# Row maxima in one, two, one chunk from the second batch on, turned in blocks, and an opening loaded through two queues

## The chip, the cores and the metric

The kernel runs on one core of a Trainium2 chip. The metric is the device time of one execution in microseconds (us), as the median of several runs. TensorE is called PE, VectorE DVE, ScalarE ACT, GpSimd POOL; SP is the engine whose queue issues most of the transfers.

## The reference

One transformer layer with normalisation after each half, on `x` of 4 batches x 512 rows x 512 features, in float32. All 16 heads (32 wide) share one key and one value head.

```python
q = rotary((x @ Wq + bq).reshape(B, T, H, HD).transpose(0, 2, 1, 3))
k, v = rotary((x @ Wk + bk)[:, None]), (x @ Wv + bv)[:, None]
attn = softmax(einsum("bhqd,bhkd->bhqk", q, k) / sqrt(HD))
x = layernorm(x + merge(attn @ v) @ Wo + bo)
hidden = sigmoid(x @ quant(w1).T) * (x @ quant(w2).T)      # 1408 wide
out = layernorm(x + hidden @ quant(w3).T)
# quant(w) = clip(round(w / (mean(abs(w)) + 1e-8)), -1, 1)
```

## The kernel before

The work is a list of 64 attention steps `(b, c, t)`: batch b, group c of four heads (NG = 4), key tile t of 128 keys. They are counted from 0 here, so batch b has steps 16b to 16b+15. A step computes the transposed scores of four heads against 128 keys in two PSUM tiles `ps` (tag `sc`, two buffers of two banks), subtracts each row's maximum with a second small matmul (`negm` against ones, adding into `ps`), takes the exponential on ACT (`es`), and one step later weighs the values (`weigh`, into `acc`). In batch 0 the denominators are also summed on PE (`count`, into the bank `den`); in later batches POOL adds them up (`total`), and DVE folds them (`part`).

The maxima must be known before the scores. So `find_maxima` computes, seven steps ahead (LEAD), the scores the other way round (`pmax`), and DVE reduces them to `mx`. In batch 0 this is `row_maxima`, two heads at a time; from batch 1 on it is `maximum`, for one head and some of its four chunks of 128 queries: a pair of chunks takes a `sc` buffer, a single chunk takes the one bank `den`. When a group's maxima are complete, `spread` turns them: PE transposes `mx` (128 x 16) into `pm`, a tile of `ps_mm` (tag `mm`, two banks), ACT and DVE split the negated maxima into two parts `m`, SP writes them to DRAM (`rows`) and reads them back as rows (`negm`).

Between the maxima, a step draws other work from a list, `fill`: in halves, the projections of later batches (`project_in`: `pk`, then `pq` for each of the four groups; after each, DVE rotates the result in four or five instructions, `turn`), the output projection (`po`) with its statistics, and the feed-forward part (`gu`, `po`, one batch behind the attention). `pace` says how much a step draws. `late` holds small jobs (`spread`, `normalize`, layer norms, stores) that `due` advances twice a step. All engines but SP's waits run their instructions in the order in which this program writes them: `InOrder` and `pin` keep it.

`quantized` goes through 66 weight tiles (33 twice): the first pass sums absolute values, the second takes a sign on ACT (`sgn`) and forms -1, 0 or 1 on DVE (into `raw`), and POOL stores them. `quantize(n)` advances it by n tiles. In steps after the 16th, the sign goes to the PSUM bank `den`.

Which form a step has is decided in the main loop: as long as the last batch isn't projected (`batches[-1].done < NC`, which holds up to step 25), it takes chunks (0, 1) and (2, 3) with all of the drawn work behind them; afterwards it takes 0, then 1 and 2, then 3, with work drawn between.

The opening issues every load on SP, in this order: two small biases, `wkv`, the four chunks of `xT` of batch 0, a part of `wq`, `cos`, `sin`, and the rest. Meanwhile PE runs WARM = 24 matmuls on ones. Line 75 is the helper that records ACT, DVE and POOL instructions, line 80 that of matmuls, line 83 that of SP's transfers, line 86 that of transposes.

Of the kernel before, what the change touches and what calls it, by code (L numbers as in the profile page):

```python
# [10 lines left out]
F32 = mybir.dt.float32  # L11
F32R = mybir.dt.float32r
BF16 = mybir.dt.bfloat16
I32 = mybir.dt.int32
AF = mybir.ActivationFunctionType
ALU = mybir.AluOpType
# [4 lines left out]
P = 128  # L21
HD = 32
# [6 lines left out]
def postln_block(  # L29
# [15 lines left out]
    nc = tc.nc  # L45
    B, T, D = x.shape
    NC = D // P
    NT = T // P
    NF = wf.shape[1]
    NG = P // HD  # L50
    SCALE = 1.0 / float(HD) ** 0.5
    W = 512
    WARM = 24

    const = ctx.enter_context(tc.tile_pool(name="const", bufs=1))
    small = ctx.enter_context(tc.tile_pool(name="small", bufs=2))
    work = ctx.enter_context(tc.tile_pool(name="work", bufs=2))
# [4 lines left out]
    dram = ctx.enter_context(tc.tile_pool(name="dram", bufs=1, space=DRAM))  # L62
    ps_sc = ctx.enter_context(tc.tile_pool(name="ps_sc", bufs=2, space=PSUM))
    ps_acc = ctx.enter_context(tc.tile_pool(name="ps_acc", bufs=1, space=PSUM))
    ps_mm = ctx.enter_context(tc.tile_pool(name="ps_mm", bufs=2, space=PSUM))

    pin = tc.keep_in_program_order
# [9 lines left out]
    act, dve, pool = InOrder(nc.scalar), InOrder(nc.vector), InOrder(nc.gpsimd)  # L77
# [4 lines left out]
    def move(out, in_):  # L82
        pin(nc.sync.dma_start(out=out, in_=in_))  # L83

    def transpose(out, in_, identity):
        pin(nc.tensor.transpose(out, in_, identity))

    ident = const.tile([P, P], F32, name="ident")
# [16 lines left out]
    bq_sb = const.tile([P, 2 * NC], F32, name="bq_sb")  # L105
    bkv_sb = const.tile([P, 2], F32, name="bkv_sb")
# [11 lines left out]

    chunks = iter([(b, c) for b in range(B) for c in range(NC)])

    def load_xT(n):

        for _ in range(n):
            b, c = next(chunks, (None, None))
            if b is not None:
                batches[b].xT.append(work.tile([P, T], F32, tag="xT", name="xT", bufs=6))
                move(batches[b].xT[c], xT[b, :, c, :])

    move(bkv_sb, bkv)
    move(bq_sb, bq)  # L130
    move(wkv_sb, wkv)
    load_xT(NC)
    move(wq_sb[0], wq[:, 0])
    move(cos_sb, cos)
    move(sin_sb, sin)
# [22 lines left out]
    def quantized():  # L158

        order = ((0, False), (1, False), (0, True), (2, False), (1, True), (2, True))
        jobs = [(m, last, f) for m, last in order for f in range(NF)]

        means = {}
        for n, (m, last) in enumerate(order):
            if not last:
                for k, step in ((2, 0), (6, 1), (10, 2)):
                    means[(n + 1) * NF + k] = (m, step)
        raws, part, row, pg, hi, waiting = {}, {}, {}, {}, {}, []  # L170

        def load(k):
            if k < len(jobs):
                m, _, f = jobs[k]

                tag, bufs = ("wd", 5) if k % 2 else ("wg", 4)
                raws[k] = wp.tile([P, W], F32, tag=tag, name="raw", bufs=bufs)
                pool.dma_start(out=raws[k], in_=wf[m, f])

        def mean(m, step):  # L180
            if step == 0:
                row[m] = small.tile([P, 1], F32, tag="row", name="row")
                dve.tensor_reduce(row[m], part[m], AX.X, ALU.add)
            elif step == 1:
                pg[m] = ps_mm.tile([P, 1], F32, tag="mm", name="pg")
                mm(pg[m], ones, row[m], True, True)
                gamma = small.tile([P, 1], F32, tag="gamma", name="gamma")
                act.activation(gamma, pg[m], AF.Identity, scale=1.0 / (NF * W * P), bias=eps_q)
                row[m] = gamma
            else:  # L190
                hi[m] = small.tile([P, 1], F32, tag="hi", name="hi")
                act.mul(hi[m], row[m], 0.5)

        AHEAD = 4
        for k in range(AHEAD):
            load(k)
        for k, (m, last, f) in enumerate(jobs):
            load(k + AHEAD)
            if k in means:
                mean(*means[k])  # L200
            raw = raws.pop(k)
            if not last:
                if f == 0:
                    part[m] = small.tile([P, NF], F32, tag="part", name="part", bufs=3)
                junk = work.tile([P, W], BF16, tag="th", name="junk")
                act.activation(junk, raw, AF.Abs, accum_out=part[m][:, f : f + 1])
            else:
                if now > PER:

                    sgn = ps_acc.tile([P, W], F32, tag="den", name="sgn")  # L210
                else:
                    sgn = work.tile([P, W], BF16, tag="th", name="sgn")
                act.activation(sgn, raw, AF.Sign, bias=hi[m])
                dve.scalar_tensor_tensor(raw, raw, hi[m], sgn, ALU.is_gt, ALU.min)
                waiting.append((kept[m][f], raw))
            if len(waiting) > 2 or k + 1 == len(jobs):
                for w, q in waiting[: 1 if k + 1 < len(jobs) else 3]:
                    pool.dma_start(out=w.bitcast(F32), in_=q)
                del waiting[:1]
            yield  # L220
# [164 lines left out]
    def spread(b, c):  # L385


        s = batches[b]
        pm = ps_mm.tile([NG * NT, P], F32, tag="mm", name="pm")
        transpose(pm, s.mx[c].rearrange("p i t -> p (i t)"), ident)  # L390
        m = small.tile([NG * NT, 2, P], F32R, tag="m", name="m")
        mH, mL = m[:, 0, :], m[:, 1, :]
        act.mul(mH, pm, -1.0)
        dve.scalar_tensor_tensor(mL, pm, -1.0, mH.bitcast(F32), ALU.mult, ALU.subtract)
        s.negm[c] = work.tile([P, T], F32R, tag="negm", name="negm", bufs=3)
        yield
        rows = dram.tile([2, NG, T], F32, tag="rows", name="rows", bufs=3)
        move(rows.rearrange("n i (t k) -> (i t) n k", k=P), m.bitcast(F32))
        yield
        for n in range(2):  # L400
            move(s.negm[c].bitcast(F32).rearrange("(i r) k -> i r k", r=HD)[:, n], rows[n])
        yield

    def scores(b, c, t):
# [372 lines left out]
    def quantize(n):  # L777
        for _ in range(n):
            next(weights, None)
# [12 lines left out]
    def due():  # L792

        nonlocal slot
        slot += 1
        for entry in list(late):
            if slot >= entry[0] and next(entry[1], "end") == "end":
                late.remove(entry)
# [13 lines left out]
    def find_maxima(k, *chunks):  # L812

        if k >= len(steps):
            return
        b, c, i = steps[k]
        if chunks[0] == 0:
            ask(k + HEADS)
            while batches[b].done <= c or (b and k not in heads):
                if batches[b].done <= c:  # L820
                    fill.one()
                else:
                    begin_middle()
                    due()
                    ask(k)
        if b == 0:
            row_maxima(b, c, i, chunks[0] // 2)
        else:
            maximum(b, c, i, chunks, heads[k])
        if i == NG - 1 and chunks[-1] == NT - 1:  # L830

            late.insert(0, (slot + (1 if now < 0 else 2), spread(b, c)))
# [22 lines left out]
    for n, (b, c, t) in enumerate(steps):  # L855
        now = n
        pace = (1.8, 3.8, 4.8, 4.6)[b]
        if t == 1 and PER <= n + NT - 1 < len(steps):
            load_q(*steps[n + NT - 1][:2])
        es = scores(b, c, t)  # L860
        if last is not None:
            weigh(*last)
        if last is not None and last[0] == 0:
            count(*last)
        last = (b, c, t, es)
        if n == NC * NT // 2:

            late.append((slot, load_x(0)))
        if t == NT - 1:
            begin = slot + 3  # L870
            late.append((begin, normalize(b, c)))
            if c == NC - 1:
                late.append((begin + 7, feed(b)))
                if b > 0:
                    late.append((slot + 6, load_x(b)))
        if batches[-1].done < NC:

            find_maxima(n + LEAD, 0, 1)
            begin_middle()
            due()  # L880
            find_maxima(n + LEAD, 2, 3)
            quantize(1)
            fill.draw(pace)
            quantize(1 if b == 0 or n % 3 == 0 else 0)
        else:
            find_maxima(n + LEAD, 0)
            fill.draw(0.4 * pace)
            find_maxima(n + LEAD, 1, 2)
            begin_middle()
            due()  # L890
            fill.draw(0.3 * pace, True)
            find_maxima(n + LEAD, 3)
            fill.draw(0.3 * pace)
        due()
# [70 lines left out]
```

## Time and profile before

| | |
|---|---|
| median of 3 runs | 672.12 us (670.8 to 674.28) |
| the profiled execution | 672.56 us, its span 670.8 us |
| mean granted TensorE clock | 0.997 |
| instructions | 9406 |
| PE, DVE, ACT, POOL busy | 644.7, 430.0, 282.8, 324.4 us |
| HBM read, written | 84.06 MB, 23.10 MB |

The span runs from the first to the last instruction. Busy times are unions; a matmul's row shows the time until its result is written, and matmuls overlap, so the distance between starts says more of PE's pace than the durations do. In a row of groups come line, engine, operation, output<-input, shapes, count, then busy us and mean ns of one, then the idle time of the engine just before and what ended it. In a row of the timeline come start, length, engine, line, operation, names, shapes, count, and in brackets the idle time before. In a row of the windows come the stretch, its length, the busy time of each engine, the granted clock, the mean share of the DMA engines, and GB/s.

### The profile page before, as it was taken

Reading aid. Unit: us, or ns where it says so; the run is one execution under the profiler, and the core shown is the slowest. Engines: PE = TensorE matmul, PEld = TensorE weight load, DVE = VectorE, ACT = ScalarE, POOL = GpSimd, SP = SyncE. Lnnn points to the kernel's source line nnn. Section 1 sums busy time; section 2 is a strip of 40 time slices with the busy share of each in tenths; the row PEclk is TensorE's granted clock in tenths of the full one; section 3 lists DMA queues with packets and bytes.
Section 4 is the critical chain, followed back from the end, with each engine's and each line's share of the span. In section 5 each row is a group of like instructions: output and inputs, shape, how many; then the busy total and the mean of one; then the engine's idle time right before and its main releaser. Section 6 shows DMA issues by size and latency. Waiting matters only on the chain.

```text
span 670.8 us, 9406 instructions
## 1 busy us (share of the span) xinstructions
PE 644.7 (96%) x3222; PEld 358.5 (53%) x3222; DVE 430.0 (64%) x619; ACT 282.8 (42%) x441; POOL 324.4 (48%) x414
## 2 busy tenths in 40 slices
PE   9989999999999989999999899999999999999995
PEld 6333333443333355665456466654555685778884
DVE  1896766587787867766666966676635553464335
ACT  1466555655443644333334445233435421234213
POOL 0615334535987776376666375576574802202000
PEclk9999999999999999999999999999999999999998
DMA  8755668688575286355132456351232364236531
GB/s 283 248 192 175 205 199 261 186 286 276 162 245 172 92 259 202 116 169 162 54 84 82 125 164 215 124 172 29 73 100 67 126 217 148 79 109 213 183 107 63
DMA packets 60671, 107.78 MB, mean 161 GB/s; under 512 B 14592, under 2 KB 15360, under 8 KB 60624
## 3 DMA queue, kind: packets, MB, share of 16 engines
q1 hardware_dynamic: 52560, 81.10, 38.5%
q0 software_dynamic: 7920, 25.96, 11.8%
q8 instruction: 25, 0.41, 0.3%
q14 instruction: 22, 0.18, 0.1%
q10 hardware_dynamic: 144, 0.13, 0.1%
HBM read 84.06 MB, written 23.10 MB: 160 GB/s over the span
## 4 chain that ended last, share of the span: by engine, by line
PE 81%; DVE 9%; DMA 4%; ACT 3%; issue 2%; SPq 1%; POOL 0%; DVEq 0%; ACTq 0%; POOLq 0%
PE gu L80 23%; PE po L80 19%; PE ps L80 11%; PE pmax L80 8%; PE acc L80 7%; PE pq L80 7%; DVE mx L75 3%; PE den L80 2%; DMA wg<-w 2%; ACT es L75 2%; PE pk L80 1%; DVE xt L75 1%; PE warm L80 1%; SPq L83 1%; DMA xT<-in_xT 1%
## 5 line engine op out<-in xcount | busy, mean ns | idle before, releaser
L75 DVE TENSOR_REDUCE mx<-pmax 128x1 f32<-128x512 f32 (+1 forms) x159 | 158.1, 1007 | 81.3 <-PE pmax L80 81.1
L75 ACT ACTIVATE es<-ps 128x1024 f32<-128x1024 f32 x128 | 124.2, 1022 | 141.9 <-PE ps L80 133.9
L80 PE MATMUL gu<-y,wg 128*128 128x512 f32 x704 | 172.9, 395 | 2.0 <-DMA wg<-w 1.1
L80 PEld LDWEIGHTS gu<-y,wg 128*128 128x128 f32 x704 | 131.1, 188 | 38.4 <-issue 4.7
L75 POOL TENSOR_TENSOR total<-total,es 128x512 f32<-128x512 f32 x96 | 123.8, 1319 | 45.2 <-ACT es L75 45.1
L80 PE MATMUL po<-wd,h 128*128 128x512 f32 x352 | 87.0, 395 | 4.2 <-DVE y L75 2.9
L75 POOL TENSOR_TENSOR total<-es 128x512 f32<-128x512 f32 x48 | 60.5, 1290 | 55.8 <-ACT es L75 55.8
L80 PE MATMUL pmax<-kr,qr 128*128 128x512 f32 x192 | 75.2, 455 | 3.7 <-ACT es L75 2.2
L80 PEld LDWEIGHTS po<-wd,h 128*128 128x128 f32 x352 | 64.9, 188 | 22.5 <-DVE y L75 4.6
L75 ACT CAST h<-hw 128x512 fp32r<-128x512 f32 x44 | 27.3, 620 | 100.7 <-DVE hw L75 100.7
L80 PE MATMUL acc<-es,v 128*32 128x512 f32 x512 | 68.2, 605 | 0.0
L80 PEld LDWEIGHTS pmax<-kr,qr 128*128 128x128 f32 x192 | 33.6, 188 | 57.0 <-ACT es L75 20.9
L75 DVE SCALAR_TENSOR_TENSOR hw<-th,gu 128x512 f32<-128x512 f32 x44 | 30.2, 687 | 46.9 <-PE gu L80 46.8
L80 PE MATMUL po<-wo_sb,ctxT 128*128 128x512 f32 x128 | 58.9, 593 | 0.3 <-DVE hw L75 0.3
L80 PE MATMUL ps<-negm,ones_r 2*128 2x512 f32 x256 | 58.2, 788 | 0.0
L75 DVE SCALAR_TENSOR_TENSOR xt<-po,xt 128x512 f32<-128x512 f32 x48 | 32.8, 684 | 38.1 <-PE po L80 38.1
L75 DVE TENSOR_TENSOR h<-hw,h 128x512 fp32r<-128x512 f32 x44 | 42.1, 957 | 21.7 <-ACT h L75 21.4
L80 PE MATMUL ps<-qT,kT 32*128 32x512 f32 x384 | 55.6, 640 | 0.0
L75 POOL DMA_DIRECT2D raw<-in_wf x66 | 36.1, 549 | 37.4 <-DMA w<-raw 26.7
L80 PE MATMUL pq<-xT,wq_sb 128*128 128x512 f32 x112 | 53.0, 601 | 1.0 <-ACT v L75 1.0
L75 ACT ACTIVATE th<-gu 128x512 f32<-128x512 f32 x44 | 26.3, 598 | 49.1 <-PE gu L80 49.0
L80 PEld LDWEIGHTS po<-wo_sb,ctxT 128*128 128x128 f32 x128 | 24.1, 189 | 22.0 <-issue 19.2
(98 smaller groups left out, 639.2 us busy)
## 6 DMA issues: line engine op xcount, KB each, us to landing
wg<-w SPq DMA_DIRECT2D x88, 256.0 KB
raw<-in_wf POOLq DMA_DIRECT2D x66, 256.0 KB, 4.6
qr<-qp SPq DMA_DIRECT2D x96, 128.0 KB
wd<-w SPq DMA_DIRECT2D x44, 256.0 KB
w<-raw POOLq DMA_DIRECT2D x33, 256.0 KB, 4.9
qp<-q SPq DMA_DIRECT2D x48, 128.0 KB
rden<-flat SPq DMA_DIRECT2D x64, 64.0 KB
xt<-in_x SPq DMA_DIRECT2D x16, 256.0 KB
```

Source lines behind the costliest of these rows:

```text
L75: return lambda *args, **kw: pin(getattr(self.engine, name)(*args, **kw))
L80: pin(nc.tensor.matmul(out, lhsT=lhsT, rhs=rhs, start=start, stop=stop))
L83: pin(nc.sync.dma_start(out=out, in_=in_))
```

## The change

Five things change.

- WARM goes from 24 to 10.
- The four opening chunks of `xT` are issued alternately by ACT's queue and SP's; the two bias loads follow on ACT's queue.
- `spread` no longer uses PE and ACT: DVE negates the 128 x 16 maxima, takes the rest, and turns both in blocks of 32 x 32 (`turned`). The rows go to DRAM as 128 pieces of 128 bytes, and `negm` is put together from pieces of 128 bytes.
- The steps' form: all steps from batch 1 on take chunk 0, then 1 and 2, then 3, with work drawn between. By the built order this affects steps 16 to 25; before and after them the steps hold the same work in the same order, but for `spread`.
- From step 17 on the sign of the quantizing goes to an SBUF buffer (`rot_a`, bfloat16) in place of the bank `den`, which the single chunks now use.

```diff
-    WARM = 24
+    WARM = 10
...
-    def load_xT(n):
+    def load_xT(n, engines=(nc.sync,)):
...
-        for _ in range(n):
+        for k in range(n):
...
-                move(batches[b].xT[c], xT[b, :, c, :])
-
-    move(bkv_sb, bkv)
-    move(bq_sb, bq)
+                pin(engines[k % len(engines)].dma_start(out=batches[b].xT[c], in_=xT[b, :, c, :]))
+
     move(wkv_sb, wkv)
-    load_xT(NC)
+    load_xT(NC, (nc.scalar, nc.sync))
+    pin(nc.scalar.dma_start(out=bkv_sb, in_=bkv))
+    pin(nc.scalar.dma_start(out=bq_sb, in_=bq))
...
-                    sgn = ps_acc.tile([P, W], F32, tag="den", name="sgn")
+                    sgn = work.tile([P, W], BF16, tag="rot_a", name="sgn", bufs=1)
...
-        pm = ps_mm.tile([NG * NT, P], F32, tag="mm", name="pm")
-        transpose(pm, s.mx[c].rearrange("p i t -> p (i t)"), ident)
-        m = small.tile([NG * NT, 2, P], F32R, tag="m", name="m")
-        mH, mL = m[:, 0, :], m[:, 1, :]
-        act.mul(mH, pm, -1.0)
-        dve.scalar_tensor_tensor(mL, pm, -1.0, mH.bitcast(F32), ALU.mult, ALU.subtract)
+        mx = s.mx[c].rearrange("p i t -> p (i t)")
+        m = small.tile([P, 2, NG * NT], F32R, tag="m", name="m")
+        turned = small.tile([P, HD], F32, tag="turned", name="turned")
+        dve.tensor_scalar(m[:, 0, :], mx, -1.0, None, ALU.mult)
+        dve.scalar_tensor_tensor(m[:, 1, :], mx, -1.0, m[:, 0, :].bitcast(F32), ALU.mult, ALU.subtract)
+        dve.transpose(turned, m.rearrange("p n k -> p (n k)").bitcast(F32))
         s.negm[c] = work.tile([P, T], F32R, tag="negm", name="negm", bufs=3)
         yield
-        rows = dram.tile([2, NG, T], F32, tag="rows", name="rows", bufs=3)
-        move(rows.rearrange("n i (t k) -> (i t) n k", k=P), m.bitcast(F32))
-        yield
+        rows = dram.tile([P // HD, 2, NG, NT, HD], F32, tag="rows", name="rows", bufs=3)
+        move(rows.rearrange("o n i t k -> (o n i t) k"), turned)
+        yield
+        to = s.negm[c].bitcast(F32).rearrange("(i r) (t o k) -> i r t o k", r=HD, t=NT, o=P // HD)
         for n in range(2):
-            move(s.negm[c].bitcast(F32).rearrange("(i r) k -> i r k", r=HD)[:, n], rows[n])
+            move(to[:, n], rows[:, n].rearrange("o i t k -> i t o k"))
...
-        if batches[-1].done < NC:
+        if b == 0:
 
             find_maxima(n + LEAD, 0, 1)
             begin_middle()
...
             find_maxima(n + LEAD, 0)
+            quantize(1)
             fill.draw(0.4 * pace)
             find_maxima(n + LEAD, 1, 2)
             begin_middle()
             due()
+            quantize(1 if n % 3 == 0 else 0)
             fill.draw(0.3 * pace, True)
```

## The prediction

> **What bounds the kernel now.** I read the page's busy shares first, then the chain that ended last, then the groups kept apart by shape, the timeline of single steps, and the windows of the opening.
>
> ```profile
> PE 644.7 (96%) x3222; PEld 358.5 (53%) x3222; DVE 430.0 (64%) x619; ACT 282.8 (42%) x441; POOL 324.4 (48%) x414
> ...
> PE 81%; DVE 9%; DMA 4%; ACT 3%; issue 2%; SPq 1%; POOL 0%; DVEq 0%; ACTq 0%; POOLq 0%
> ```
>
> TensorE (PE) is busy for 96% of the span and carries 81% of the chain: what leaves its queue, or makes it wait, moves the end; other engines matter only where they hold it up.
>
> ```profile
> L80 PE MATMUL pmax<-kr,qr 128*128 128x512 f32 x192 | 75.2, 455 | 3.7 <-ACT es L75 2.2 <-DVE mx L75 1.0
> L86 PE MATMUL pm<-ident,mx 128*16 128x128 f32 x16 | 4.4, 273 | 1.3 <-DVE mx L75 1.3
> L75 DVE SCALAR_TENSOR_TENSOR m<-pm,m 16x128 fp32r<-16x128 f32 x16 | 4.3, 270 | 0.0
> ```
>
> These groups are touched. Waits are small throughout; the 16 `pm` transposes cost PE 273 ns each before what follows them is counted.
>
> **Part 1, the opening: -3.4 us.** In the windows (PE first, then the loads; last the granted clock, DMA share, GB/s):
>
> ```profile
> 1.50:7.30 5.80, 5.80 (x27) 5.80 (x28) 0.00 (x0) 0.71 (x2) 0.16 (x3) 1.00 0.74 177
> 7.30:9.80 2.50, 2.50 (x24) 2.50 (x24) 0.00 (x0) 0.00 (x0) 0.00 (x0) 1.00 1.03 354
> 9.80:13.30 3.50, 3.50 (x11) 1.59 (x10) 0.00 (x0) 0.00 (x0) 0.00 (x0) 1.00 1.05 406
> ```
>
> The 24 warming matmuls are 48 passes, and the first real one, `pk`, starts at 9.77 with no wait shown: it stands behind the warming. Passes come every 0.215 us up to 7.3 (5.80/27) and every 0.104 us after it (2.50/24), although the granted clock reads 1.00: PE runs at half pace first. Ten warming matmuls are 20 passes and end near 5.9. The data: by the windows of one microsecond some 0.9 MB had landed by 7.0 and 1.6 MB by 9.0. `wkv` and the first `xT` chunk are 0.52 MB, so about 5.1, all four chunks 1.3 MB, about 8.2. The two small bias loads go off SP's front, so everything is issued 0.9 us earlier (`wkv` from 1.64 to 0.73): 4.2 and 7.3. The last chunk is needed 2.6 us after `pk` starts, so data aren't late. ScalarE's four issues, at about 0.45 us each by SP's rows, are hidden: its first real work starts at 13.40 now. `pk` thus moves from 9.77 to 5.9, 3.8 us. Until about 7.3 it runs at half pace, which loses 0.7 us; if the pace doubles earlier, nothing. I take -3.4. Bounds: -3.8, and -0.4 if all of `pk` (3.44 us now) runs at half pace.
>
> [...]
>
> **Part 2, the first turned maxima: -0.3.** At 37 us VectorE (DVE) sets the pace: PE's `pm` waits 1.26 us for `mx`, the next maxima come late, and DVE idles 0.49 us before 38.39. That gap goes; two more small DVE instructions come. Nearest rows: 160 ns (128x1 product), 246 (reciprocal 128x16), 233 (block transpose 32x64). Three for one of 270 ns is +0.2 to +0.5. Net -0.3 (0 to -0.4).
>
> **Part 3, the other transposes: -5.6.** After batch 0's opening, four lie in batch 0, three in steps 16 to 25 (part 4), eight later. Step 28, without, takes 244.52 to 251.61, 7.09 us; step 29, with the same matmuls and `pm`, 251.61 to 259.41, 7.80: 0.71 more, for `pm` also takes one of two PSUM banks and the next `gu` waits (0.28). The last is followed by a wait of 0.68. At 0.6 each: 4.8. In batch 0 the next matmul starts 0.03 to 0.21 after `pm`: 0.2 each, 0.8. DVE's extra 0.2 to 0.5 is hidden in the late steps, where it idles 1.2 to 4 us (6.58 busy of 7.80 in step 29), and mostly in batch 0 (0.1 to 1.1 idle); without that cover it costs up to 0.6 there. Bounds: 12 x 0.27 less 0.6 = 2.6, and 6.5; a loss is excluded, since PE's own time goes in any case. The longer DMA route (128 pieces of 128 bytes) is hidden: the maxima leave at 258.42, are fetched at 262.72 and needed at 273.6; three times that latency fits.
>
> [...]
>
> **Part 4, steps 16 to 25: +5.1, a loss.** Only these ten change their chunks; later steps had one, two, one already. A step now, then one of the later kind:
>
> ```profile
> 171.89 0.81 PE L80 MATMUL ps<-negm,ones_r 2*128 2x512 f32 x4
> 172.63 1.07 PE L80 MATMUL acc<-es,v 128*32 128x512 f32 x8
> 173.80 0.73 PE L80 MATMUL pmax<-kr,qr 128*128 128x512 f32 x2
> 174.72 0.73 PE L80 MATMUL pmax<-kr,qr 128*128 128x512 f32 x2 [0.18 <-ACT es L75]
> 175.29 1.88 PE L80 MATMUL pq<-xT,wq_sb 128*128 128x512 f32 x4
> ...
> 245.82 1.07 PE L80 MATMUL acc<-es,v 128*32 128x512 f32 x8
> 246.81 0.50 PE L80 MATMUL pmax<-kr,qr 128*128 128x512 f32 x1
> 247.16 2.02 PE L80 MATMUL gu<-y,wg 128*128 128x512 f32 x8
> 249.02 0.63 PE L80 MATMUL pmax<-kr,qr 128*128 128x512 f32 x2
> 249.48 1.98 PE L80 MATMUL gu<-y,wg 128*128 128x512 f32 x8
> 251.30 0.39 PE L80 MATMUL pmax<-kr,qr 128*128 128x512 f32 x1
> ```
>
> Gains: `acc` and maxima take 2.66 us (172.63 to 175.29) against 0.99+0.35+0.46+0.31 = 2.11, less seams 0.5 a step; nine steps 4.5. Three `pm` at 0.35: 1.0. Two waits (0.38 on `xT`, 0.35 on `v`) vanish under new ones: 0.7. Together 6.2.
>
> Losses: DVE's queue. Now the maxima are reduced before the rotation of the projection:
>
> ```profile
> 174.57 2.36 DVE L75 TENSOR_REDUCE mx<-pmax 128x2 f32<-128x1024 f32 x2 [0.29 <-PE pmax L80]
> 176.85 0.74 DVE L75 SCALAR_TENSOR_TENSOR raw<-raw,hi,sgn 128x512 f32<-128x512 f32 x1
> 177.50 0.74 DVE L75 SCALAR_TENSOR_TENSOR a<-pq,bq_sb,cos_sb 128x512 f32<-128x512 f32 x1
> ```
>
> Afterwards, by the built order, the fill between chunk 0 and the pair puts the rotation ahead of the pair's reduce in steps 16 to 19. The pair's bank of `sc` is also the one that the next step's second `ps` needs, and behind that `ps` stands all of PE. If the fill ends at F, the rotation runs from F+0.2 for 2.9 us (177.50 to 180.44) and the reduce 1.2: free at F+4.3. PE reaches the second `ps` at F+2.9 (pair 0.46, another fill half 1.8, chunk 3 0.32, first `ps` 0.28), or F+1.1 without that half. Step 16: 1.4. Step 17 rotates `pk`, after `kv` (0.68) and for 3.6 us: free at F+5.7, 2.8. Step 18, with `pv`: 1.0. Step 19, no second half: 3.2. Also, in step 16 chunk 0 takes the `den` bank, which ScalarE's `sums` copy frees: 159.36 now, behind a sign of 0.75 then, so 160.1; PE is there at 158.4: 1.7. In steps 20, 21 and 24 chunk 3's reduce stands behind statistics and `part` or `m`: 0.4 each, 1.2. Together 11.3. Net +5.1. Bounds: -0.5 if half of the waits come, +10 below. The signs' move to SBUF costs ScalarE 0.03 us each (693 ns into PSUM, 720 into SBUF) on an engine busy 42%; one buffer as before.
>
> **Sum.** -3.4 -0.3 -5.6 +5.1 = -4.2 on the profiled execution's 672.56 (span 670.8 and 1.76 around it): 668.4. That execution is 0.44 over the median 672.12, so **667.9**. Half a per cent, 3.4 us, is about what a measurement can tell from no change.
>
> **Rivals.**
> - *The rotation waits half vanish* (part 4 at -0.5): 662.3. For it: PE had only 0.2 to 0.65 us of idle in each of these steps. Against: both queues are strictly in order. 0.17.
> - *The opening brings little* (-0.4), PE staying at half pace because it stops after the warming, that is, the shorter warming doesn't do what it says: 670.9. Against: the data are there. 0.13.
> - *Slower: the one shared bank.* Chunk 0 of the next step waits for chunk 3's reduce too. If that also slips behind a rotation in 16 to 19, 4 x 2.9 = 11.6 more: 679.5. It decides from 7.6 us more. For it: DVE is busy 7.96 of 8.50 us in step 18 now. Against: the built order has that reduce directly after the pair's, or after one sign product. 0.15.
>
> **Numbers.** The forecast has 0.55, its own range 665.5 to 670.5; three quarters of it lie below 668.7, so 0.41 faster and 0.14 same. Faster 0.41+0.17 = 0.58; same 0.14+0.13 = 0.27; slower 0.15. Reaching from the first rival to half way to the third, with 2 in 10 outside: 663.0 to 674.5.
>
> **What would show it.** `pk` starting near 6 and `pq` 3 us earlier (part 1); step 29 near 7.1 (part 3); in steps 17 to 20 PE's `ps` waiting for `mx` by 1 to 3 us, `pmax` 1.7 us in step 16 (part 4). No such `ps` waits, or a `pk` at half pace for over 3 us, would make it wrong.

## The result, and the profile after

The changed kernel takes 684.04 us (median of 6 runs) against 671.66 us for the kernel before beside it. The ratio of the two is 1.0157, with a 95% interval of 1.0124 to 1.0191: it is slower by 1.6%, where 667.9 us was forecast and 674.5 was the upper end of the range. Ratios, here and below, are taken over all fast runs and not from the two medians; one run of the six, 689.55 us, was slow and is left out of the ratio. The profiled execution took 683.53 us, its span 681.8, at a mean granted clock of 0.982.

From the page of the changed kernel: the busy shares, the granted clock in 40 slices, and the chain by engine.

```profile
PE 650.2 (95%) x3178; PEld 359.6 (53%) x3178; DVE 453.7 (67%) x661; ACT 279.4 (41%) x425; POOL 327.3 (48%) x414
...
PEclk9999998999779989999999999999999999999998
...
PE 76%; DVE 15%; ACT 3%; DMA 2%; issue 2%; SPq 1%; POOL 1%; ACTq 0%; DVEq 0%; POOLq 0%
```

Two things are new. The chain runs through VectorE for 15% instead of 9%, and `PEclk`, which before was nines in all slices but the last, has dips. Before:

```profile
PEclk9999999999999999999999999999999999999998
```

A slice is 17.05 us: the first dip lies at 102 to 119 us (step 10), the two sevens at 170 to 205 (steps 17 to 20), the last but the end's at 239 to 256 (steps 25 and 26). The list of TensorE's waits in the changed kernel (us in total, how many, the longest) gives the names:

```profile
PE ps L80 <- DVE mx L75: 8.0, 5, 3.2
PE pmax L80 <- DVE mx L75: 5.9, 7, 1.6
...
PE pmax L80 <- ACT sums L75: 1.5, 1, 1.5
```

These are the kinds of wait that part 4 forecast. The group of the maxima's matmuls, which idled 3.7 us before, mostly for `es`, idles 7.2 now, for `mx`:

```profile
L80 PE MATMUL pmax<-kr,qr 128*128 128x512 f32 x192 | 83.9, 493 | 7.2 <-DVE mx L75 5.7
```

The rows that part 4 did not forecast are on VectorE; the groups of the changed kernel (count, then busy us, mean ns):

```profile
L75 DVE SCALAR_TENSOR_TENSOR raw<-raw,hi,sgn 128x512 f32<-128x512 f32 x33 | 33.0, 1011 | 1.8 <-ACT sgn L75 1.8
L75 DVE TENSOR_SCALAR m<-mx 128x16 fp32r<-128x16 f32 x16 | 9.7, 609 | 0.0
L75 DVE SCALAR_TENSOR_TENSOR m<-mx,m 128x16 fp32r<-128x16 f32 x16 | 6.9, 429 | 0.5
L75 DVE STREAM_TRANSPOSE turned<-m 128x32 f32<-128x32 f32 x16 | 3.4, 211 | 0.6
```

The signs' product in the kernel before:

```profile
L75 DVE SCALAR_TENSOR_TENSOR raw<-raw,hi,sgn 128x512 f32<-128x512 f32 x33 | 24.1, 738 | 0.4 <-ACT sgn L75 0.4
```

It takes 1011 ns in the mean against 738 before, and the two `m` instructions on 16 columns take 609 and 429 ns, where the shortest of them take 159 and 174.

The table below says where the time went. A step begins with its first `ps` matmul; each figure is the length of a stretch of steps in the profiled execution, less that of the kernel before, in us. "Half" is how long the record shows TensorE's granted clock at 0.5 within steps 16 to 26. e1 to e14 are the experiments. The columns of steps come from one profiled execution, which can lie away from its median: 5.5 us above it in e11, 3.3 above in e9, 2.8 below in e7, 2.6 below in e12.

| run | ratio (95%) | before step 0 | 0-9 | 10 | 11-15 | 16-26 | 27-62 | half |
|---|---|---|---|---|---|---|---|---|
| changed kernel | 1.0157 (1.0124-1.0191) | -4.2 | -0.4 | +4.0 | +0.4 | +18.7 | -7.0 | 17.1 |
| e1 opening, turned | 0.9943 (0.9915-0.9971) | -4.1 | +1.2 | +3.3 | +0.4 | +2.1 | -6.4 | 0 |
| e2 part 4 alone | 1.0321 (1.0271-1.0370) | +0.1 | 0 | 0 | 0 | +24.7 | -1.6 | 20.5 |
| e3 signs alone | 1.0030 (1.0009-1.0051) | -0.7 | 0 | 0 | 0 | +1.7 | -0.3 | 1.3 |
| e4 short sums | 1.0149 (1.0096-1.0203) | -4.6 | -0.4 | +1.8 | +0.4 | +18.5 | -7.1 | 23.9 |
| e5 pair first | 1.0128 (1.0094-1.0163) | -4.3 | -0.4 | +5.1 | +0.2 | +16.4 | -6.6 | 13.7 |
| e6 waits filled | 1.0218 (1.0158-1.0277) | -3.7 | +2.9 | +4.2 | +0.4 | +20.7 | -5.7 | 13.7 |
| e7 turned alone | 1.0006 (0.9976-1.0036) | -1.5 | -0.4 | +3.5 | +0.5 | +1.4 | -5.7 | 0 |
| e8 m off VectorE | 0.9859 (0.9824-0.9893) | -3.5 | -1.4 | -0.1 | -0.3 | +0.5 | -4.8 | 0 |
| e9 = e4 and e5 | 0.9999 (0.9979-1.0020) | -3.7 | +2.8 | +3.5 | +0.4 | +6.4 | -5.7 | 3.4 |
| e10 opening alone | 0.9969 (0.9954-0.9984) | -4.2 | 0 | 0 | 0 | +1.0 | -0.1 | 0 |
| e11 sent at once | 0.9899 (0.9868-0.9930) | -3.7 | +1.8 | -0.1 | -0.3 | +2.8 | -2.5 | 3.4 |
| e12 chunks at best | 1.0003 (0.9979-1.0028) | -4.2 | -1.5 | -0.1 | -0.3 | +9.8 | -5.8 | 3.4 |
| e13 = e4, waits filled | 1.0081 (1.0049-1.0113) | -4.0 | -0.4 | +3.3 | +0.4 | +10.6 | -5.6 | 6.8 |
| e14 = e4 again | 1.0162 (1.0093-1.0231) | -3.5 | -0.4 | +1.7 | +0.5 | +16.9 | -6.4 | 20.5 |

In the changed kernel's row the opening and the late steps bring 11.2, and steps 10 and 16 to 26 cost 22.7. Of the 18.7 in steps 16 to 26, 15.5 lie in steps 16 to 25, whose chunks changed, and 3.1 in step 26.

### The profile page after: what moved, and what is told of

It is laid out like the page before. It is cut to its first block, busy times and chain, and to the rows that moved or that the text cites. A ratio compares the mean times of both kernels' runs of the same rounds, so it can differ in the third digit from the quotient of the medians.

```text
span 681.8 us, 9337 instructions
## 1 busy us (share of the span) xinstructions
PE 650.2 (95%) x3178; PEld 359.6 (53%) x3178; DVE 453.7 (67%) x661; ACT 279.4 (41%) x425; POOL 327.3 (48%) x414
## 4 chain that ended last, share of the span: by engine, by line
PE 76%; DVE 15%; ACT 3%; DMA 2%; issue 2%; SPq 1%; POOL 1%; ACTq 0%; DVEq 0%; POOLq 0%
PE gu L80 22%; PE po L80 17%; PE ps L80 12%; PE pmax L80 8%; PE acc L80 8%; PE pq L80 5%; DVE mx L75 5%; PE den L80 2%; DVE part L75 1%; DVE raw L75 1%; ACT es L75 1%; SPq L83 1%; DVE pq L75 1%; DMA bq_sb<-in_bq 1%; DVE xt L75 1%
## 5 line engine op out<-in xcount | busy, mean ns | idle before, releaser
L80 PE MATMUL pmax<-kr,qr 128*128 128x512 f32 x192 | 83.9, 493 | 7.2 <-DVE mx L75 5.7
L75 POOL TENSOR_TENSOR total<-es 128x512 f32<-128x512 f32 x48 | 61.9, 1321 | 57.5 <-ACT es L75 57.5
L80 PE MATMUL acc<-es,v 128*32 128x512 f32 x512 | 70.8, 626 | 0.0
L80 PE MATMUL ps<-qT,kT 32*128 32x512 f32 x384 | 64.0, 649 | 6.5 <-DVE mx L75 6.4
L80 PEld LDWEIGHTS pmax<-kr,qr 128*128 128x128 f32 x192 | 35.8, 192 | 64.1 <-issue 20.7
L80 PE MATMUL ps<-negm,ones_r 2*128 2x512 f32 x256 | 64.4, 780 | 0.0
L80 PE MATMUL pq<-xT,wq_sb 128*128 128x512 f32 x112 | 54.4, 612 | 0.6 <-ACT v L75 0.6
```

The source lines that it names most:

```text
L75: return lambda *args, **kw: pin(getattr(self.engine, name)(*args, **kw))
L80: pin(nc.tensor.matmul(out, lhsT=lhsT, rhs=rhs, start=start, stop=stop))
```

## The experiments

### The parts by themselves: e1, e2, e3

The edit of e1 to the changed kernel takes part 4 out; e2 is the kernel before with only that part; e3 is the kernel before with only the signs' move, the last two lines.

```diff
-        if b == 0:
+        if batches[-1].done < NC:
...
             find_maxima(n + LEAD, 0)
-            quantize(1)
...
-            quantize(1 if n % 3 == 0 else 0)
...
-                    sgn = work.tile([P, W], BF16, tag="rot_a", name="sgn", bufs=1)
+                    sgn = ps_acc.tile([P, W], F32, tag="den", name="sgn")
```

> The kernel before with the new opening and the block-turned maxima, but with the old chunks and the signs in PSUM. Theory (VectorE waits for GpSimd when it reads only SBUF, and a stall of TensorE can cost half pace after it): -4.2 for the opening, -0.3 in batch 0, +4.0 in step 10 (m<-mx again over 1 us beside the xt sums, then half pace for 3.4 us), -6.4 in the late steps, about -1 in steps 16 to 25: 8 less than before, 664. Rival, the forecast's parts 1 to 3 without that wait: 9.3 less and nothing in step 10, 662.4. If the loss of the changed kernel lay in these parts, it would be over 672.

> The kernel before with part 4 alone: chunks one, two, one from step 16 on and the signs in SBUF. Theory: raw<-raw,hi,sgn takes 1.3 us and more beside GpSimd's sums, the second ps waits for mx, TensorE runs at half pace for 3.4 or 6.8 us after the longest of these waits; 16 to 19 more than before, 689. Rival, each wait at its own length as forecast, with no half pace: 6.1 more, 678.

> The kernel before with one change: from step 17 on the signs go into SBUF; chunks in pairs as before. Theory: about ten products raw<-raw,hi,sgn grow from 0.74 to 1.3 us and more where GpSimd is summing; VectorE was busy 7.96 of 8.50 us in step 18, so a part of these 7 us shows: 2 to 6 more than before, with more if a wait of TensorE reaches 1.6 us and brings half pace. Rival, the forecast's price (0.03 us of ScalarE each): no difference, within 1 us.

e1 came to 668.95 us, 0.6% faster than before: the loss isn't in the opening or the turned maxima. It was 5 us over the expectation: in its profile half pace fell into step 0 as well, step 17 waited 0.90 us for a load of `xT`, and `m` delayed step 26. e2 came to 694.26 us, 3.2% slower, with half pace for 20.5 us in steps 16 to 26: part 4 loses by itself, and more than expected. In these steps it lost even 6 us more than the changed kernel, which holds the same edit; a wait of 3.89 us of `pq` for `kT` in step 17 stands in e2 alone, and what brings it was not looked for. So the parts do not simply add up. e3 was 0.3% slower, some 2 us, at the lower end of what was expected. In its profile nearly all of that lies in step 26; in steps 16 to 25 it lost 0.1. But its rows show plainly that VectorE is held. VectorE of e3 in step 19, and GpSimd beside it:

```profile
184.88 1.71 DVE L75 SCALAR_TENSOR_TENSOR raw<-raw,hi,sgn 128x512 f32<-128x512 f32 x1
```

```profile
182.32 5.40 POOL L75 TENSOR_TENSOR total<-total,es 128x512 f32<-128x512 f32 x4
```

The product waits inside its own row for one of the four sums to end. With the sign in PSUM, from step 17 on, it took 0.73 to 0.75 us in every step of the kernel before, beside the same sums. So a hold alone cost little here, 0.1 us over steps 16 to 25, as long as TensorE didn't need what stood behind it.

### Two causes, each enough: e4, e5, e9

e4 takes away GpSimd's long sums and leaves the order; e5 changes the order of VectorE's queue and leaves the sums; e9 does both. e4 and e9, and later e13 and e14, leave out 480 of the 512 columns of batch 1's sums, so they only probe the time and don't compute the layer.

```diff
# e4
...
-                        pool.tensor_tensor(s.total[j][:, i, :], s.total[j][:, i, :], es[j][:, i, :], ALU.add)
+                        some = slice(0, 32 if b == 1 else T)
+                        pool.tensor_tensor(s.total[j][:, i, some], s.total[j][:, i, some], es[j][:, i, some], ALU.add)
# e5
-            fill.draw(0.4 * pace)
+            if batches[-1].done == NC:
+                fill.draw(0.4 * pace)
             find_maxima(n + LEAD, 1, 2)
+            if batches[-1].done < NC:
+                fill.draw(0.4 * pace)
```

> The changed kernel, but GpSimd's sums total<-total,es in batch 1 take 32 of 512 columns (the rest of the total is set to one), so GpSimd holds nothing long there; order and number of instructions otherwise the same. Theory: the products raw<-raw,hi,sgn are back at 0.74 us, the waits of the second ps shrink below 1.6 us, half pace goes from steps 16 to 26: 10 to 14 less than the changed kernel, near 671 to 674. Rival, the order of VectorE's queue alone (rotation ahead of the pair's reduce): waits of 2 to 3 us and half pace stay, over 680.

> The changed kernel with one thing moved: while the last projections run (steps 16 to 25) the pair of chunks comes ahead of the first fill, so its reduce stands ahead of the rotation in VectorE's queue. Theory (after the run with short sums, the order of the queue and the half pace after a stall are the cause, and GpSimd's hold on VectorE is small): the waits of the second ps for mx in steps 18 and 20 and the half pace there go, steps 16 to 26 lose 12 to 15 less, 669 to 672. Rival, the move from pairs to one, two, one as such or the signs in SBUF: within 4 of the changed kernel, 680 to 684.

> The changed kernel with both edits at once: the pair of chunks ahead of the first fill in steps 16 to 25, and GpSimd's sums of batch 1 on 32 of 512 columns (the rest of the total is set to one). Theory (two causes, either of which alone keeps the waits: the rotation ahead of the pair's reduce, and the signs' product held by GpSimd): neither wait of over 3 us is left, the products take 0.74 us; what stays is the wait for sums in step 16 (1.5), one for the bank of chunk 3 in step 18 (some 2) and those for y and statistics; steps 16 to 26 take 6 to 11 more than before instead of 16 to 19, so 670 to 675. Rival, the one, two, one chunks as such with their shared bank: still 15 or more, over 679.

The first theory, that GpSimd's hold is the cause, fell with e4: the products were back at 0.74 us but for two, and steps 16 to 26 still lost 18.5, 14.2 of it in steps 16 to 25. A part is new with the short sums: in step 26 the second `m` is held behind GpSimd's split of `q`, and a single chunk waits 3.4 us, where it waited 1.56 in the changed kernel. VectorE, then TensorE in e14, which is e4 once more:

```profile
242.63 1.99 DVE L75 SCALAR_TENSOR_TENSOR m<-mx,m 128x16 fp32r<-128x16 f32 x1
```

```profile
248.29 0.79 PE L80 MATMUL pmax<-kr,qr 128*128 128x512 f32 x1 [3.37 <-DVE mx L75]
```

The second theory, that the order alone is the cause, fell with e5: 681.25 us, still +16.4, 13.5 of it in steps 16 to 25. In e5 the signs' product stood ahead of the pair's reduce, and it waited out the three sums that were left of four. VectorE, GpSimd and TensorE of e5 in steps 19 and 20:

```profile
190.20 4.96 DVE L75 SCALAR_TENSOR_TENSOR raw<-raw,hi,sgn 128x512 f32<-128x512 f32 x1
195.08 1.21 DVE L75 TENSOR_REDUCE mx<-pmax 128x2 f32<-128x1024 f32 x1
```

```profile
188.91 4.95 POOL L75 TENSOR_TENSOR total<-total,es 128x512 f32<-128x512 f32 x4
```

```profile
191.90 1.13 PE L80 MATMUL ps<-qT,kT 32*128 32x512 f32 x4
196.35 1.22 PE L80 MATMUL ps<-qT,kT 32*128 32x512 f32 x2 [3.33 <-DVE mx L75]
```

The four sums follow each other at once, and the product, which starts beside the second, ends 1.3 us after the last. So the second `ps` waits 3.3 us, as it does in the changed kernel behind the rotation. e9, with both gone, came to +6.4 there, 672.51 us in all, with half pace for only 3.4 us in these steps: within its expectation, but for the wait of 3.35 us in step 26, which that had excluded. In steps 16 to 25 it lost 2.2. The two causes hide each other; either alone keeps steps 16 to 25 at 12.6 us (e14) or more over the kernel before.

### Half pace is a price of its own: e6, e13, e14

TensorE of the changed kernel in step 18, VectorE behind which it waits, and three windows (granted clock third from the end):

```profile
173.01 1.13 PE L80 MATMUL ps<-qT,kT 32*128 32x512 f32 x4
176.30 1.05 PE L80 MATMUL ps<-qT,kT 32*128 32x512 f32 x2 [2.16 <-DVE mx L75]
```

```profile
170.03 1.48 DVE L75 SCALAR_TENSOR_TENSOR raw<-raw,hi,sgn 128x512 f32<-128x512 f32 x1 [0.34 <-ACT sgn L75]
171.43 0.74 DVE L75 SCALAR_TENSOR_TENSOR a<-pk,bkv_sb,cos_sb 96x512 f32<-96x512 f32 x1
...
173.61 1.38 DVE L75 TENSOR_TENSOR kT<-a,pk 96x512 f32<-96x512 f32 x2
175.02 1.22 DVE L75 TENSOR_REDUCE mx<-pmax 128x2 f32<-128x1024 f32 x1
```

```profile
171.00:176.50 5.50, 3.34 (x14) 1.24 (x14) 5.35 (x10) 0.39 (x1) 3.91 (x4) 1.00 0.43 124
176.52:183.35 6.83, 6.83 (x20) 2.17 (x17) 3.06 (x6) 2.66 (x3) 3.92 (x4) 0.50 0.32 102
183.35:190.00 6.65, 6.51 (x33) 2.47 (x31) 5.94 (x9) 2.55 (x5) 5.96 (x7) 1.00 0.39 123
```

The reduce frees the bank at 176.2, 3.3 us after TensorE began the tile before it. Then the clock is at 0.50 for 6.83 us. To part the stall from this, the first `ps` tile's matmuls are repeated, so that TensorE works where it waited and nothing comes sooner:

```diff
-            for i in range(2):
-                rows = ts(2 * j + i, HD)
-                mm(ps[:, i, :], s.kT[rows, ts(t, P)], s.q[c][rows, :], True, False)
+            again = {18: 2, 20: 2}.get(now, 0) if j == 0 else 0      # e6: {10: 1, 18: 2, 20: 3}
+            for k in range(again + 1):
+                for i in range(2):
+                    rows = ts(2 * j + i, HD)
+                    mm(ps[:, i, :], s.kT[rows, ts(t, P)], s.q[c][rows, :], True, k < again)
```

> The changed kernel, with the first ps tile's matmuls done twice in step 10, three times in step 18 and four times in step 20 (each repeat begins the sum anew, some 1.05 us), so that TensorE works where it waited. Nothing else is moved and nothing comes sooner. Theory (half pace is a price of its own for the stall): no or less half pace near 115, 177 and 197; 4 to 8 less than the changed kernel, 676 to 680. Rival, the stall costs its own length only: no gain, 0 to 3 more than the changed kernel, 684 to 687.

e6 missed: 688.08 us, above both ranges. Step 18 did shorten, from 13.95 to 10.70 us, without half pace; but in step 19 a signs' product now fell among four sums (5.09 us), step 20 stalled for 3.0 us beyond the filling, and half pace followed for 10.2 us. So the test was made again without GpSimd's long sums, with e4 once more as the base.

> The changed kernel with GpSimd's sums of batch 1 on 32 of 512 columns (the rest of the total is set to one), and the first ps tile's matmuls done three times over in steps 18 and 20, so that TensorE works through the two waits of 2.2 and 2.4 us of the run with short sums alone. Nothing comes sooner by that. Theory (half pace after a stall is a price of its own): no half pace near 175 and 196, steps 18 and 20 at some 10.5 us instead of 13.8 and 13.5; 5 to 7 less than with short sums alone, 675 to 677. Rival (the stall costs its own length): no gain, 682 or more.

> The run with short sums alone (batch 1's sums on 32 of 512 columns) once more, on the chip of the run above, as its base: within 1 of 682.

TensorE in step 18, of e14 first and then of e13:

```profile
171.59 1.13 PE L80 MATMUL ps<-qT,kT 32*128 32x512 f32 x4
174.88 1.22 PE L80 MATMUL ps<-qT,kT 32*128 32x512 f32 x2 [2.16 <-DVE mx L75]
...
175.89 1.06 PE L80 MATMUL ps<-qT,kT 32*128 32x512 f32 x2
```

```profile
172.57 2.85 PE L80 MATMUL ps<-qT,kT 32*128 32x512 f32 x12
175.86 0.70 PE L80 MATMUL ps<-qT,kT 32*128 32x512 f32 x2 [0.45 <-DVE mx L75]
...
176.39 0.59 PE L80 MATMUL ps<-qT,kT 32*128 32x512 f32 x2
```

In both the second tile starts 3.29 us after the first. In e14 what follows runs at half pace (1.01 us to the next pass), in e13 at full pace (0.53). Step 18 takes 13.84 and 10.70 us, step 20 13.53 and 10.40, and the medians are 682.17 and 677.14: 5 us, the lower end of what was expected, for work that brings nothing but a busy TensorE. Over steps 16 to 26 the two differ by 6.3 us and by 13.7 us of half pace: 0.46 us lost for each us of it. e4, the same kernel as e14, gives a third point: in steps 16 to 25 the losses are 6.35 us without half pace (e13), 12.62 with 13.65 us of it (e14) and 14.20 with 17.07 us (e4), again 0.46.

### The m instructions, and a kernel that is faster: e7, e8, e11

> The kernel before with the block-turned maxima alone. Theory: -0.3 in batch 0, 0 to +4 in step 10 (m<-mx beside the xt sums, 1.1 us twice, then half pace or not), +0.5 in step 14, about +1 in steps 17 and 26 where m and the signs' products stand in VectorE's queue, -6.4 in the late steps: 1 to 6 less, 668. Rival, the forecast's parts 2 and 3: 5.9 less, 666.

The turned maxima alone came to no difference (ratio 1.0006), where 1 to 6 us less was expected: of what they bring in the late steps, 5.7 us in the profile, 4.8 is lost in step 10 and in steps 16 to 26. Step 10 of the changed kernel, VectorE, then GpSimd, then TensorE:

```profile
110.62 1.08 DVE L75 TENSOR_SCALAR m<-mx 128x16 fp32r<-128x16 f32 x1
111.74 1.19 DVE L75 SCALAR_TENSOR_TENSOR m<-mx,m 128x16 fp32r<-128x16 f32 x1
112.96 0.21 DVE L75 STREAM_TRANSPOSE turned<-m 128x32 f32<-128x32 f32 x1
113.10 1.18 DVE L75 TENSOR_REDUCE mx<-pmax 128x2 f32<-128x1024 f32 x1
```

```profile
110.42 2.48 POOL L75 TENSOR_TENSOR xt<-xt,bo_sb 128x512 f32<-128x512 f32 x2 [9.91 <-DMA xt<-in_x]
```

```profile
114.33 0.70 PE L80 MATMUL ps<-room,kT 32*128 32x512 f32 x2 [1.66 <-DVE mx L75]
```

Each `m` ends 0.03 us after one of the two `xt` sums. Together they take 2.3 us instead of 0.34, the reduce behind them comes late, TensorE stalls 1.66 us, and half pace follows for 3.4. e8 takes both instructions off VectorE; it is e1 with:

```diff
-        dve.tensor_scalar(m[:, 0, :], mx, -1.0, None, ALU.mult)
-        dve.scalar_tensor_tensor(m[:, 1, :], mx, -1.0, m[:, 0, :].bitcast(F32), ALU.mult, ALU.subtract)
+        if now < 0:
+            dve.tensor_copy(m[:, 0, :], mx)
+            dve.tensor_tensor(m[:, 1, :], mx, m[:, 0, :].bitcast(F32), ALU.subtract)
+        else:
+            halves(m[:, 0, :], m[:, 1, :], mx)      # copy on ScalarE, difference on GpSimd
+            yield
...
-    pool.memset(ones_r.bitcast(F32), 1.0)
+    pool.memset(ones_r.bitcast(F32), -1.0)
```

> The kernel of the first run (opening and turned maxima, old chunks, signs in PSUM), but from step 0 on the split of the maxima is done by ScalarE and GpSimd (a copy and a difference), and VectorE turns the block one slot later; the sign of the maxima is put into ones_r. Theory (what is left over in step 10, 17 and 26 of the first run comes from the two m instructions, which take up to 1.2 us each on VectorE beside GpSimd's sums): step 10 is back at 6.4 and no half pace near 117, 3 to 5 less than the first run's 669, 664 to 666. Rival (the stall in step 10 has another cause): within 1.5 of 669.

e8 came to 662.87 us, a ratio of 0.9859 (0.9824 to 0.9893): faster than both kernels, under the 664 to 666 expected, and the lowest median of this study. Its distance to e1 is not all the `m` instructions': some 1.5 us of it is the half pace in step 0 of e1's profile. Step 10 is back at 6.33 us, no half pace lies in the span between the opening and the end, and steps 16 to 26 are 0.5 over the kernel before. GpSimd fits the difference in between two sums, in its own queue:

```profile
111.45 0.21 POOL L75 TENSOR_TENSOR m<-mx,m 128x16 fp32r<-128x16 f32 x1
111.63 1.26 POOL L75 TENSOR_TENSOR xt<-xt,bo_sb 128x512 f32<-128x512 f32 x1
```

> The opening, the turned maxima with their split on ScalarE and GpSimd, chunks and signs as before the change; the turned block is now sent in the slot in which it is turned. Theory: in the run without this the maxima came 0.8 us late in step 28 (ps waits for negm); that goes, and so do 0.5 to 1.5 us: 661.5 to 662.5, 1.4 to 1.6% less than before. Rival (SP's queue waits for the turned block and holds up the loads behind it): over 663.

e11 (one `yield` between the turning and the sending left out after step 0) missed: 664.75 us, where its rival lies. Its profile, taken in the slowest of its six runs (670.27 us), has half pace for 6.8 us in step 0, a wait of `pk` for `xT` (1.59 us) and one of `gu` for `wg` (2.45). Whether its runs are slower than e8's for the edit or for where half pace falls is not settled; the intervals overlap.

### The opening alone, and the chunks at their best: e10, e12

> The kernel before with the opening alone: ten warming matmuls, two queues. Theory and forecast: pk starts near 5.9 instead of 9.8 and what follows moves with it, 3.4 to 4.1 less than before, 668. Rival: the shorter warming leaves TensorE at half pace for a part of pk, or step 0's stall of 0.95 us falls so that half pace follows, 0 to 2 less, 670 to 672.

e10 came to 669.35 us, 0.3% faster (0.2 to 0.5), between the expectation and its rival. In the profile step 0 starts 4.2 us earlier; 1.0 us is given back in step 17, where TensorE is now ahead of a load:

```profile
164.27 2.24 PE L80 MATMUL pk<-xT,wkv_sb 128*128 128x512 f32 x4 [1.34 <-DMA xT<-in_xT]
```

> The kernel of the run above with chunks one, two, one from step 16 on, the pair ahead of the first fill, and the signs left in PSUM, in the bank that the single chunks use. So none of VectorE's products reads only SBUF and the pair's reduce stands ahead of the rotation. Theory: the waits for the single chunks' bank are left (sums 1.5 in step 16, chunk 3's reduce behind the rotation of pk in step 18, chunk 0 behind the signs' product), with half pace after the longest; 4 to 9 more than the run above, 666 to 671. Rival, the forecast's gains (0.5 a step from fewer matmul seams): 658 to 661.

e12, with no instruction of VectorE held in these steps and the pair ahead of the rotation, was still 9.8 us over the kernel before in steps 16 to 26, and 672.83 us in all, 1.8 over its expectation. The waits of TensorE in e12:

```profile
PE pmax L80 <- DVE raw L75: 6.2, 5, 3.5
PE pmax L80 <- DVE mx L75: 4.7, 8, 1.0
```

The bank that signs and single chunks now share is late. So the form one, two, one cost more in these steps than its 0.5 us a step of seams in every variant tried. One thing was never varied: the place of the signs' product, right behind chunk 0, in VectorE's queue.

## Why the prediction was wrong

Part 4 is the step that failed: +5.1 us was forecast for steps 16 to 25, and +15.5 was measured there, with 3.1 more in step 26. Its mechanism was right. The gain came: step 24, where nothing waits, is 0.70 us shorter (0.5 forecast). The waits came where it put them: 1.54 us for `sums` in step 16 (1.7 forecast), then for the second `ps` 0.71 (1.4), 2.16 (2.8), under 0.4 (1.0) and 3.21 (3.2; with short sums 2.43, so this agreement is partly luck). Three terms were wrong.

- **A stall was priced at its own length.** Half pace was weighed for the opening alone. With 0.46 us for each us at half pace (e13, e14 and e4), the 13.7 us of it in steps 16 to 25 cost 6.3.
- **The signs' move was priced on ScalarE, not on VectorE.** "The signs' move to SBUF costs ScalarE 0.03 us each" left out that the product then reads only SBUF. With the price of half pace taken out, steps 16 to 25 lose 9.2 in the changed kernel and 6.3 with short sums (e4, e13 and e14): 2.9 us for the hold. This is an estimate from single profiles. The trace of before had shown it in another group, which the forecast didn't look at, 128x512 as the product is; the group and one of its instructions, then GpSimd beside it, all of the kernel before:

```profile
L75 DVE TENSOR_TENSOR h<-hw,h 128x512 fp32r<-128x512 f32 x44 | 42.1, 957 | 21.7 <-ACT h L75 21.4
```

```profile
499.35 1.79 DVE L75 TENSOR_TENSOR h<-hw,h 128x512 fp32r<-128x512 f32 x1 [1.82 <-ACT h L75]
```

```profile
498.04 4.24 POOL L75 TENSOR_TENSOR total<-total,es 128x512 f32<-128x512 f32 x3 [1.19 <-ACT es L75]
```

  Both inputs of this instruction lie in SBUF. It takes 0.65 to 0.69 us where GpSimd idles and up to 1.79 beside its sums. A mean of 957 with such a spread is the sign to look for.
- **One of the small waits was too small.** 0.4 us each was put for the chunk 3 of steps 20, 21 and 24; the single chunks behind them waited 0.32 in step 21, 1.47 in 22 and 1.39 in 25. In step 22 it is the hold again (0.38 with short sums); in step 25 the reduce stands behind a rotation, and 1.36 stays. With the hold and half pace out, steps 16 to 25 stand at 6.3 where 5.1 was forecast. Step 26, with a wait of 1.56 and half pace, was not in the forecast at all.

The held products of the changed kernel take 1.3 to 1.8 us, once 3.4, instead of 0.74, beside GpSimd instructions of 1.26 to 1.72 us; what GpSimd loses by it was not measured.

Part 3's mechanism was right for the late steps: -5.2 over steps 29, 33, 37, 41, 45, 49, 53 and 57, where -4.8 was forecast for these eight transposes; step 29 takes 7.09 us. The term that failed is VectorE's extra of 0.2 to 0.5 us for three instructions ("without that cover it costs up to 0.6 there"), taken from rows that GpSimd had not held. The three took 2.5 us in step 10 instead of one of 0.27, and that step lost 4.0. Rows with small pieces were there to read: in both kernels `flat<-few` moves pieces of 128 bytes and less (16 issues of 8 KB). TensorE of the changed kernel waits for `negm` nowhere, so the longer route stayed hidden, as forecast.

Part 1 had the right mechanism and nearly the right size. TensorE's opening in the changed kernel:

```profile
4.22 1.84 PE L80 MATMUL warm<-ones 128*128 128x128 f32 x8
5.89 3.60 PE L80 MATMUL pk<-xT,wkv_sb 128*128 128x512 f32 x8
9.33 3.60 PE L80 MATMUL pq<-xT,wq_sb 128*128 128x512 f32 x8
```

`pk` starts at 5.89 and `pq` 3.44 us later, so `pk` has full pace at once; step 0 is 4.2 us earlier (3.7 forecast with part 2). The full pace is this run's luck. In e6, e8, e9, e11 and e14, with the same opening, the first two passes of `pk` are 0.86 us apart instead of 0.44, and `pq` follows after 3.9 to 4.2 us: the 0.7 us that the forecast took off for half pace. Over the twelve profiles with this opening step 0 comes 3.5 to 4.6 us earlier. Part 2's 0.3 can't be told from such a spread: in e3, where nothing changes before step 0, it comes 0.7 earlier. And e10's median gains 2.7 us, not 3.4, for a part is given back in step 17.

The wait of 0.96 us of `pmax` for `es` in step 0 stands in all sixteen profiles. Half pace followed it in e1, e6, e9 and e11 alone. All four have the new opening, but so have eight others, so whether the opening has a part in it is open; the gain is less certain than the profile of the changed kernel shows.

Of the rivals, the slower one named the single chunks' bank. In steps 17 to 19 the changed kernel has no such wait, for there the second `ps` waits; behind a rotation it came only in steps 25 and 26 (1.39 and 1.56), and in e5 in step 18 (3.40). So it is luck that this rival's 679.5 lies nearest to the result. Every sign that the forecast named came (`pk` near 6, step 29 near 7.1, the waits for `mx` and `sums`): they tested the mechanism and not the price.

## What to carry to other kernels

Where TensorE is busy for 96%, price a new wait by what may follow it: here the step with a stall of 2.2 us became 5.5 us longer. When an operand moves from PSUM to SBUF, look up who else is reading SBUF at that time, above all GpSimd (here the product went from 738 to 1011 ns in the mean), and look in the trace for a group of the same kind whose mean lies well above its least. And when undoing one suspected cause changes nothing, undo two together before dropping either: here either of two was enough for most of the loss.

## What the runs showed of the hardware

- Half pace came in pieces of 3.41, 6.83 or 10.24 us. In the changed kernel it began at 115.08, 176.52, 197.00 and 251.62 us; the starts lie 61.44, 20.48 and 54.62 us apart, which is 18, 6 and 16 times 3.41.
- In the sixteen profiles all 17 stalls of TensorE over 2 us between 20 and 620 us were followed by half pace, and 18 of 127 stalls between 0.9 and 2 us. In the changed kernel those of 1.56, 1.66, 2.16 and 3.21 us were followed by it and those of 1.54 us and less were not; the 1.6 us in the expectations of e3 and e4 is an estimate that fits this one profile. The wait of 0.96 us in step 0 was followed by it in four profiles of sixteen, so the same wait was cheap in one profile and dear in another. What decides it was not shown.
- The length of the half pace did not go by that of the stall: 2.16 us and 3.21 us brought 6.83 us of it each in the changed kernel, and 0.96 us brought 6.8 in e9.
- An instruction of VectorE that GpSimd held ended, as a rule, 0.55 us (128x512) or 0.03 us (128x16) after the instruction it waited for, and could be held through three of GpSimd's sums in a row (3.38 us in the changed kernel, 4.96 in e5). The first `m`, with one SBUF operand, was held as well (1.08 us in step 10 instead of 0.16). A product with one operand in PSUM (0.73 to 0.75 us) and the block transpose with one SBUF operand (0.21, at 500.17 us in the changed kernel and at 111.70 in e8) were not held beside such sums.
